# Layer 0 of a four-layer graph network: project the features before they are aggregated, and add a bias as one BF16 product

## The chip, the cores and the metric

The kernel runs on one core of a Trainium2 chip. The metric is the device time of one execution in microseconds (us); lower is better. Three executions of the kernel before took 3515.82, 3516.83 and 3521.38 us; the median is 3516.83 us. Engines are named as in the profile: PE (TensorE, matrix products), PEld (its weight loads), DVE (VectorE), ACT (ScalarE), POOL (GpSimd) and SP (SyncE, whose queue starts all the transfers here).

## The reference

The network has 3327 nodes with 256 features, a dense FP32 adjacency matrix with about 1% nonzero entries, and four residual layers, each followed by a layer norm without weights. Only layer 0 and the entry of layer 1 are touched:

```python
x = _layernorm(x + _L0(x, adj, W))          # W is 256 x 512
def _L0(features, adj, W):
    deg = adj.sum(axis=1, keepdims=True) + 1.0
    neigh = adj @ features / deg
    return jnp.concatenate([features, neigh], axis=-1) @ W.T

x = _layernorm(x + _L1(x, adj, gcn_w, gcn_b, ...))
def _L1(...):
    h = jax.nn.relu(adj @ x @ gcn_w + gcn_b)   # then a layer norm, then a Mamba block over the nodes
```

Layer 2 is a graph attention layer, layer 3 two diffusion steps with top-p attention. Layer 0 is the same as features W1 + (adj features / deg) W2, with W1 and W2 the two halves of W transposed, and since a row's division by deg commutes with a product from the right, also features W1 + (adj (features W2)) / deg.

## The kernel before

The nodes are padded to 26 tiles of 128 (nt = 26). The kernel gives each engine one list of instructions, worked off in order. The framework makes these lists before the run: it goes through the program with estimated durations and takes the ready instruction of highest priority, where earlier in the program means higher priority unless the program says otherwise (high_priority, issue_after, keep_in_program_order). So loads for a later stage can be listed, and run, during an earlier one, if their memory is free. All transfers wait in the one list of SP.

**Layer 0** (lines 162 to 189). xa holds the features of all tiles with a 257th column of ones, so that the product with an adjacency row of tiles also gives the row sums. For each of the 26 output tiles, aggregate() (line 110) multiplies 26 adjacency blocks of 128 x 128 (at, loaded in two pieces of 13 blocks, four buffers) with xa into a PSUM tile acc of 257 columns (line 120). An FP32 product shows as two PE instructions in the profile, so that is 52 instructions a tile. The first tile also loads xa itself, four tiles at a time between the adjacency pieces (lines 115 to 118). Then a chain follows: DVE adds 1 to the row sum (176), takes the reciprocal (177) and scales acc (179) into m; PE transposes m (105), ACT copies it to mt (107); PE multiplies the transposed features xt and mt with the four 128-row blocks of w0 into po (line 183, eight instructions of 256 columns); DVE adds the features (186); layernorm() writes tile it of X0, which is the tile F. After tile 13, projections() prepares small weights of layer 3.

**Layer 1, graph convolution** (convolve(), from line 319). For each of 26 tiles, PE multiplies 26 adjacency blocks with X0 (line 333, 52 instructions); ACT copies the sum (341), PE transposes it (344), ACT copies it (346), PE multiplies with gcn_w (349, four instructions), and adds the bias as a product of a row of ones with the row gcn_b (350): contraction length 1, FP32, two instructions. Then come relu on ACT (353), a norm on ACT and POOL (308 to 316, 360), and a transposition into hT (370, 372). The first three tiles are done ahead of the Mamba block's first chunk, four more ahead of its 16 state steps (pump()), and the other 19 are spread over the later state steps by quotas of work units that the program computes.

**Layer 1, Mamba block.** Chunks of up to 512 nodes; the head of a chunk projects hT (489), does a short convolution (492, 499), silu, and step sizes (513 to 552); 16 state steps with scans on DVE (line 274 in the profile, for all DVE and POOL instructions with a fixed order), exponentials on ACT (281), products on POOL, and sums on PE (624). scratch() hands out the four rotating buffers of a pool that the heads use; the loads of the attention vectors (238) also use it.

Of the kernel before, what the change touches and what calls it, by code (L numbers as in the profile page):

```python
# [9 lines left out]
F32 = mybir.dt.float32  # L10
BF16 = mybir.dt.bfloat16
I32 = mybir.dt.int32
AF = mybir.ActivationFunctionType
ALU = mybir.AluOpType
# [4 lines left out]
P = 128  # L19
D = 256  # L20
EPS = 1e-5
JH = 13
J0 = 4
# [7 lines left out]
NG = DI // P  # L31
DS = 16
DTR = 16
# [14 lines left out]
def gnn_kernel(ctx: ExitStack, tc: tile.TileContext, n: int, a: dict, out: bass.AP):  # L48
    nc = tc.nc
    nt = -(-n // P)  # L50
# [6 lines left out]
    ident = consts.tile([P, P], F32, name="ident")  # L57
# [4 lines left out]
    rdeg = consts.tile([P, nt], F32, name="rdeg")  # L62

    X = keep.tile([P, nt, D], F32, name="X")
# [5 lines left out]
    def load(pool, name):  # L70
        t = pool.tile(list(a[name].shape), F32, name=name)
        nc.sync.dma_start(t, a[name])
        return t
# [20 lines left out]
    def layernorm(dst, y):  # L94
        mv = small.tile([P, 2], F32, name="mv")
        stats(mv, y)
        rs = small.tile([P, 1], F32, name="rs")
        rstd_of(rs, mv[:, 1:2])
        standardize(dst, y, mv[:, 0:1], rs)

    def transposed(pool, psum, src, name):

        pt = psum.tile([P, D // P, P], F32, name="ps")
        for k in range(D // P):
            nc.tensor.transpose(pt[:, k, :], src[:, k * P:(k + 1) * P], ident)
        t = pool.tile([P, D // P, P], F32, name=name)
        nc.scalar.copy(t, pt)
        return t

    def aggregate(atp, psum, it, rhs, cols, jh=JH, source=None):  # L110

        acc = psum.tile([P, cols], F32, name="acc")
        for j0 in range(0, nt, jh):
            m = min(jh, nt - j0)
            if source is not None:
                nc.sync.dma_start(rhs[:, j0:j0 + m, :D], source[:, j0:j0 + m, :])
            at = atp.tile([P, jh, P], F32, name="at")
            nc.sync.dma_start(at[:, :m, :], a["adjT"][it][:, j0:j0 + m, :])
            for j in range(m):
                nc.tensor.matmul(acc, at[:, j, :], rhs[:, j0 + j, :],  # L120
                                 start=(j0 + j == 0), stop=(j0 + j == nt - 1))
        return acc
# [19 lines left out]
    def projections(wpool, psum):  # L142
        w1 = load(wpool, "W1")
        w2 = load(wpool, "W2")
        for h in range(2):
            nc.sync.dma_start(wkq[h][:, :, h * DA:(h + 1) * DA], a["W3"])

        for k in range(2):
            pt = psum.tile([DA, P], F32, name="ps")
            nc.tensor.transpose(pt, w1[:, k, :], ident)  # L150
            wt = wpool.tile([DA, P], F32, name=f"w1t{k}")
            nc.scalar.copy(wt, pt)
            pw = psum.tile([P, DA], F32, name="ps")
            nc.tensor.matmul(pw, wt, w2, start=True, stop=True)
            for h in range(2):
                nc.scalar.copy(wkq[h][:, k, (1 - h) * DA:(2 - h) * DA], pw)

    with tc.tile_pool(name="l1b", bufs=1) as wpool, tc.tile_pool(name="l1at", bufs=2) as l1at:
# [3 lines left out]
        with tc.tile_pool(name="l0", bufs=1) as pool, tc.tile_pool(name="l0w", bufs=2) as work, \  # L162
                tc.tile_pool(name="l0at", bufs=4) as atp, \
                tc.tile_pool(name="l0p", bufs=2, space=PSUM) as psum:
            xa = pool.tile([P, nt, D + 1], F32, name="xa")
            nc.vector.memset(xa[:, :, D:], 1.0)
            for it in range(nt):
                if it:
                    acc = aggregate(atp, psum, it, xa, D + 1)
                else:  # L170
                    acc = aggregate(atp, psum, it, xa, D + 1, J0, a["x"])
                    w0 = load(pool, "w0")
                xt = work.tile([P, D // P, P], F32, name="xt")
                nc.sync.dma_start(xt, a["xT"][:, :, it * P:(it + 1) * P])
                deg = small.tile([P, 1], F32, name="deg")
                nc.vector.tensor_scalar_add(deg, acc[:, D:D + 1], 1.0)
                nc.vector.reciprocal(rdeg[:, it:it + 1], deg)
                m = work.tile([P, D], F32, name="m")
                nc.vector.tensor_scalar_mul(m, acc[:, :D], rdeg[:, it:it + 1])
                mt = transposed(work, psum, m, "mt")  # L180
                po = psum.tile([P, D], F32, name="po")
                for k in range(4):
                    nc.tensor.matmul(po, xt[:, k, :] if k < 2 else mt[:, k - 2, :], w0[:, k, :],
                                     start=(k == 0), stop=(k == 3))
                y = work.tile([P, D], F32, name="y")
                nc.vector.tensor_add(y, po, xa[:, it, :D])
                layernorm(X0[:, it, :], y)
                if it == nt // 2:
                    projections(pool, psum)


        with tc.tile_pool(name="l1aw", bufs=1) as cwork, tc.tile_pool(name="l1c", bufs=2) as ch, \
# [6 lines left out]
            def scratch():  # L199
                return tmp.tile([P, NG, 3 + WC], F32, name="t")  # L200

            gw = load(wpool, "gcn_w")

            w_dt = wpool.tile([32 * (NG - 1) + DTR, P + D + P], F32, name="w_dt")
            gb, one = w_dt[0:1, P:P + D], w_dt[0:1, P + D:]
            nc.sync.dma_start(gb, bass.AP(tensor=a["gcn_b"].tensor, offset=a["gcn_b"].offset, ap=[[0, 1], [1, D]]))
            nc.vector.memset(one, 1.0)

            def by_channel(name):
                t = wpool.tile([P, D // P], F32, name=name)  # L210
                nc.sync.dma_start(t, bass.AP(tensor=a[name].tensor, offset=a[name].offset, ap=[[1, P], [P, D // P]]))
                return t
# [190 lines left out]
            def duty(c, s):  # L403


                m, n, b = tiles_of(c), tiles_of(c + 1), tiles_of(c - 1)
                p = plan(c)
                return 4 * m * (2 if s == 0 else 1) + 24 * (1 <= s <= b) + 16 * len(gates(c, s)) \
                    + 4 * n * len(p["project"].get(s, ())) + 8 * n * (s == p["mixed"]) + 2 * n * len(p["sizes"].get(s, ()))

            def tiles_of(c):
                return (ends[c] - starts[c]) // P if 0 <= c < nch else 0
# [272 lines left out]
            for k, (c, s) in enumerate(states):  # L685
                w = us[c].shape[2]
                m = tiles_of(c)
# [59 lines left out]
                if c and 9 <= s < 9 + tiles_of(c - 1):  # L747
                    rs, nb = plus[:2]
                    i = s - 9
                    x = X[:, starts[c - 1] // P + i, :]  # L750
# [29 lines left out]
                part = min(q, max(0, SPLIT - 4 * m - duty(c, s) // 2)) if len(uses) > 1 else q  # L780
# [7 lines left out]
            m = tiles_of(nch - 1)  # L788
# [5 lines left out]
            for i in range(m):  # L794
                it = starts[nch - 1] // P + i
# [16 lines left out]
    with tc.tile_pool(name="l3", bufs=1) as pool, tc.tile_pool(name="l3d", bufs=1, space=DRAM) as dram:  # L812
# [90 lines left out]
        with tc.tile_pool(name="l2c", bufs=1) as cpool:  # L903
# [5 lines left out]
            with tc.tile_pool(name="l2a", bufs=1) as wpool, \  # L909
# [4 lines left out]
                m = wpool.tile([P, 2], F32, name="m")  # L914
# [5 lines left out]
                one = wpool.tile([2, 1], F32, name="one")  # L920
# [14 lines left out]
                for j0 in range(0, nt, 4):  # L935
                    m = min(4, nt - j0)
# [678 lines left out]
```

## Time and profile before

| | |
|---|---|
| Median of three runs | 3516.83 us |
| Profiled execution, its own time | 3519.38 us |
| Its span, first to last instruction | 3517.5 us |
| Mean granted PE clock | 0.970 |
| PE busy, share of span | 3235.5 us, 92% |
| DVE busy | 2370.4 us, 67% |
| ACT busy | 1740.6 us, 49% |
| POOL busy | 932.8 us, 27% |
| Read from HBM | 294.36 MB |
| PE in layer 0 | from 5.58 us to about 355 us |
| Graph convolutions of layer 1 (line 333) | from 354.1 us to about 1136 us |

A busy share is a mean over stages that have different limits, so the stages are read one at a time. "Idle before" in a group of instructions is the time that the engine stood still just ahead of them, with the instruction that ended most of it. PE records overlap: a product's record is longer than the distance to the next product, and the distance (here called the pitch) is what a stream of products costs.

### The profile page before, as it was taken

Reading aid. Unit: us, or ns where it says so; the run is one execution under the profiler, and the core shown is the slowest. Engines: PE = TensorE matmul, PEld = TensorE weight load, DVE = VectorE, ACT = ScalarE, POOL = GpSimd, SP = SyncE. Lnnn points to the kernel's source line nnn. Section 1 sums busy time; section 2 is a strip of 40 time slices with the busy share of each in tenths; the row PEclk is TensorE's granted clock in tenths of the full one; section 3 lists DMA queues with packets and bytes.
Section 4 is the critical chain, followed back from the end, with each engine's and each line's share of the span. In section 5 each row is a group of like instructions: output and inputs, shape, how many; then the busy total and the mean of one; then the engine's idle time right before and its main releaser. Section 6 shows DMA issues by size and latency. Waiting matters only on the chain. (4 is left out here: it accounts for less than half of the span.)

```text
span 3517.5 us, 43266 instructions
## 1 busy us (share of the span) xinstructions
PE 3235.5 (92%) x15597; PEld 2540.3 (72%) x15597; DVE 2370.4 (67%) x5245; ACT 1740.6 (49%) x2751; POOL 932.8 (27%) x942
## 2 busy tenths in 40 slices
PE   9999988988888766999899999999997999999996
PEld 7888766676676555888677878787775777777775
DVE  1111177999999997777454544444434999999996
ACT  0000356767667675111133333333336888888883
POOL 0000054666665653121100000000001243333332
PEclk9999998999999888999899999999999999999998
DMA  7443334334443222344321212121212112222220
GB/s 248 139 140 110 102 109 112 101 119 106 106 119 91 66 58 92 126 140 145 95 66 56 65 49 65 48 67 47 67 47 74 55 56 67 68 70 61 70 65 16
DMA packets 147577, 307.99 MB, mean 88 GB/s; under 512 B 19570, under 2 KB 68850, under 8 KB 147218
## 3 DMA queue, kind: packets, MB, share of 16 engines
q1 hardware_dynamic: 147346, 305.06, 29.7%
q8 instruction: 126, 2.06, 0.2%
q14 instruction: 105, 0.86, 0.1%
HBM read 294.36 MB, written 10.65 MB: 87 GB/s over the span
## 5 line engine op out<-in xcount | busy, mean ns | idle before, releaser
L274 POOL TENSOR_TENSOR h<-du,row 128x2048 f32<-128x2048 f32 (+1 forms) x110 | 465.7, 4233 | 339.3 <-DVE hc L274 270.8
L274 DVE TENSOR_TENSOR_SCAN h<-dA,carry,h 128x512 f32<-128x512 f32 (+1 forms) x384 | 448.7, 1220 | 19.8 <-ACT dA L281 19.7
L281 ACT ACTIVATE dA<-t,A_log 128x512 f32<-128x512 f32 (+1 forms) x448 | 292.3, 658 | 146.4 <-DVE h L274 143.4
L1058 PE MATMUL acc<-F,at 128*128 128x256 f32 x1352 | 353.5, 387 | 1.0 <-ACT q L832 0.6
L1091 PE MATMUL acc<-X,wt 128*128 128x256 f32 x1352 | 343.5, 390 | 10.5 <-ACT wt L1089 10.2
L1091 PE MATMUL acc<-G,wt 128*128 128x256 f32 x1352 | 336.8, 392 | 6.4 <-ACT wt L1022 5.9
L1091 PEld LDWEIGHTS acc<-X,wt 128*128 128x128 f32 x1352 | 242.6, 189 | 105.3 <-issue 41.3
L120 PE MATMUL acc<-xa,at 128*128 128x257 f32 x1352 | 308.6, 382 | 5.6 <-DMA at<-in_adjT 5.6
L1058 PE MATMUL acc<-X,at 128*128 128x256 f32 x1352 | 308.4, 381 | 0.0
L967 PE MATMUL acc<-F,at 128*128 128x257 f32 x1352 | 303.6, 381 | 1.2 <-DMA U<-in_U 1.2
L333 PE MATMUL cb<-F,at 128*128 128x256 f32 x1196 | 294.0, 394 | 7.4 <-ACT hn L353 4.5
L1091 PEld LDWEIGHTS acc<-G,wt 128*128 128x128 f32 x1352 | 250.1, 193 | 67.0 <-ACT wt L1022 36.8
L1103 DVE MAX8 cand<-e 128x8 f32<-128x128 f32 x676 | 142.2, 278 | 229.0 <-ACT e L1044 217.4
L1058 PEld LDWEIGHTS acc<-F,at 128*128 128x128 f32 x1352 | 237.9, 190 | 75.3 <-issue 50.2
L120 PEld LDWEIGHTS acc<-xa,at 128*128 128x128 f32 x1352 | 255.7, 191 | 42.4 <-issue 5.5
L1058 PEld LDWEIGHTS acc<-X,at 128*128 128x128 f32 x1352 | 252.9, 191 | 40.2 <-issue 7.0
L967 PEld LDWEIGHTS acc<-F,at 128*128 128x128 f32 x1352 | 253.4, 190 | 36.8 <-issue 1.4
L333 PEld LDWEIGHTS cb<-F,at 128*128 128x128 f32 x1196 | 228.8, 197 | 59.4 <-issue 14.3
L624 PE MATMUL y<-ident,hc 128*128 128x128 f32 x1664 | 229.7, 291 | 42.9 <-DVE hc L274 42.3
L624 PEld LDWEIGHTS y<-ident,hc 128*128 128x128 f32 x1664 | 204.5, 151 | 82.5 <-DVE hc L274 59.3
L274 DVE TENSOR_TENSOR hc<-h,row 128x2048 f32<-128x2048 f32 (+2 forms) x114 | 242.8, 2131 | 11.0 <-PE y L624 4.3
L1089 ACT COPY wt<-tp 128x512 f32<-128x512 f32 (+1 forms) x182 | 93.5, 557 | 309.2 <-PE tp L1087 309.0
(352 smaller groups left out, 5264.1 us busy)
## 6 DMA issues: line engine op xcount, KB each, us to landing
at<-in_adjT SPq DMA_DIRECT2D x102, 832.0 KB, 4.6
at<-in_adjT SPq DMA_DIRECT2D x260, 320.0 KB, 2.9
row<-bc SPq DMA_DIRECT2D x80, 512.0 KB, 5.1
at<-in_adjT SPq DMA_DIRECT2D x52, 576.0 KB, 4.0
at<-in_adjT SPq DMA_DIRECT2D x26, 512.0 KB, 3.8
row<-bc SPq DMA_DIRECT2D x32, 384.0 KB, 5.0
xt<-in_xT SPq DMA_DIRECT2D x26, 128.0 KB, 4.1
qd<-q SPq DMA_DIRECT2D x104, 32.0 KB, 1.9
```

What stands on the lines that cost most here:

```text
L120: nc.tensor.matmul(acc, at[:, j, :], rhs[:, j0 + j, :], start=(j0 + j == 0), stop=(j0 + j == nt - 1))
L274: return lambda *x, **k: tc.keep_in_program_order(op(*x, **k))
L281: decays.append(op(*x, **k))
L333: ten.matmul(acc, at[:, j % JC, :], X0[:, j, :], start=(j == 0), stop=(j == nt - 1))
L624: x = ten.matmul(y[:, g * P:(g + 1) * P], h[:, g, i * P:(i + 1) * P], ident, is_transpose=True, start=(first and g == 0), stop=(last and g ...
L967: nc.tensor.matmul(acc, at[:, j, :], F[:, j0 + j, :], start=(j0 + j == 0), stop=(j0 + j == nt - 1))
L1058: nc.tensor.matmul(acc, at[:, j, :], rhs[:, j0 + j, :], start=(j0 + j == 0), stop=(j0 + j == nt - 1))
L1089: copy(wt[:, :m, :], pt[:, :m, :])
L1091: nc.tensor.matmul(acc, wt[:, j, :], rhs[:, j0 + j, :], start=(j0 + j == 0), stop=(j0 + j == nt - 1))
L1103: nc.vector.max(cand[:, s * 8:(s + 1) * 8], z[:, s * SEG:(s + 1) * SEG])
```

## The change

In layer 0, w0 is loaded first, and the identity is added to the two diagonal 128 x 128 blocks of its first half, so that features (W1 + I) already contains the residual. Then a loop ahead of the aggregation loads the transposed features xT in pieces of four tiles (xt, two buffers of 4 KB per partition) and multiplies each tile once with both halves of w0, 512 columns at a time, into a PSUM tile po. DVE copies the first 256 columns to X (a tile that layer 1 overwrites later), ACT copies the other 256 to xa. The aggregation now works on the projected xa; after it, one DVE instruction scales acc by the reciprocal degree and adds X, and the layer norm follows. The features in their plain layout are no longer loaded, and per tile the transposition, its copy, the four products with w0 and the load of xt are gone.

In layer 1, the bias row is split into three BF16 parts, whose sum is the FP32 row, held in partitions 0, 32 and 64 of a tile gb of 65 partitions that is zero elsewhere; the row of ones becomes a 65 x 128 BF16 tile. The line ten.matmul(acc, one, gb, ...) is unchanged in its text and is now a BF16 product of contraction length 65. The split is done once by DVE: two memsets, six copies and two subtractions, on a scratch() buffer into which the bias is loaded for all 65 partitions.

```diff
-    def aggregate(atp, psum, it, rhs, cols, jh=JH, source=None):
+    def aggregate(atp, psum, it, rhs, cols, jh=JH):
 
         acc = psum.tile([P, cols], F32, name="acc")
         for j0 in range(0, nt, jh):
             m = min(jh, nt - j0)
-            if source is not None:
-                nc.sync.dma_start(rhs[:, j0:j0 + m, :D], source[:, j0:j0 + m, :])
             at = atp.tile([P, jh, P], F32, name="at")
             nc.sync.dma_start(at[:, :m, :], a["adjT"][it][:, j0:j0 + m, :])
...
             xa = pool.tile([P, nt, D + 1], F32, name="xa")
             nc.vector.memset(xa[:, :, D:], 1.0)
+            w0 = load(pool, "w0")
+            for k in range(2):
+                own = w0[:, k, k * P:(k + 1) * P]
+                nc.vector.tensor_add(own, own, ident)
+            for j0 in range(0, nt, J0):
+                m = min(J0, nt - j0)
+                xt = work.tile([P, D // P, J0 * P], F32, name="xt")
+                nc.sync.dma_start(xt[:, :, :m * P], a["xT"][:, :, j0 * P:(j0 + m) * P])
+                for i in range(m):
+                    po = psum.tile([P, 2, D], F32, name="po")
+                    for k in range(2):
+                        nc.tensor.matmul(po, xt[:, k, i * P:(i + 1) * P], w0[:, k::2, :], start=(k == 0), stop=(k == 1))
+                    nc.vector.tensor_copy(X[:, j0 + i, :], po[:, 0, :])
+                    nc.scalar.copy(xa[:, j0 + i, :D], po[:, 1, :])
             for it in range(nt):
-                if it:
-                    acc = aggregate(atp, psum, it, xa, D + 1)
-                else:
-                    acc = aggregate(atp, psum, it, xa, D + 1, J0, a["x"])
-                    w0 = load(pool, "w0")
-                xt = work.tile([P, D // P, P], F32, name="xt")
-                nc.sync.dma_start(xt, a["xT"][:, :, it * P:(it + 1) * P])
+                acc = aggregate(atp, psum, it, xa, D + 1)
                 deg = small.tile([P, 1], F32, name="deg")
                 nc.vector.tensor_scalar_add(deg, acc[:, D:D + 1], 1.0)
                 nc.vector.reciprocal(rdeg[:, it:it + 1], deg)
-                m = work.tile([P, D], F32, name="m")
-                nc.vector.tensor_scalar_mul(m, acc[:, :D], rdeg[:, it:it + 1])
-                mt = transposed(work, psum, m, "mt")
-                po = psum.tile([P, D], F32, name="po")
-                for k in range(4):
-                    nc.tensor.matmul(po, xt[:, k, :] if k < 2 else mt[:, k - 2, :], w0[:, k, :],
-                                     start=(k == 0), stop=(k == 3))
                 y = work.tile([P, D], F32, name="y")
-                nc.vector.tensor_add(y, po, xa[:, it, :D])
+                nc.vector.scalar_tensor_tensor(y, acc[:, :D], rdeg[:, it:it + 1], X[:, it, :],
+                                               op0=ALU.mult, op1=ALU.add)
                 layernorm(X0[:, it, :], y)
...
-            w_dt = wpool.tile([32 * (NG - 1) + DTR, P + D + P], F32, name="w_dt")
-            gb, one = w_dt[0:1, P:P + D], w_dt[0:1, P + D:]
-            nc.sync.dma_start(gb, bass.AP(tensor=a["gcn_b"].tensor, offset=a["gcn_b"].offset, ap=[[0, 1], [1, D]]))
+            w_dt = wpool.tile([32 * (NG - 1) + DTR, P], F32, name="w_dt")
+            rows3 = 2 * 32 + 1
+            gb, one = wpool.tile([rows3, D], BF16, name="gb"), wpool.tile([rows3, P], BF16, name="one")
+            nc.vector.memset(gb, 0.0)
             nc.vector.memset(one, 1.0)
+            rest, part = scratch()[:rows3, 0, :D], wpool.tile([rows3, D], BF16, name="part")
+            nc.sync.dma_start(rest, bass.AP(tensor=a["gcn_b"].tensor, offset=a["gcn_b"].offset, ap=[[0, rows3], [1, D]]))
+            for k in range(3):
+                nc.vector.tensor_copy(part, rest)
+                nc.vector.tensor_copy(gb[32 * k:32 * k + 1, :], part[32 * k:32 * k + 1, :])
+                if k < 2:
+                    nc.vector.tensor_sub(rest, rest, part)
```

## The prediction

> **What bounds the kernel now.** I read the page's slices first. PE is at 9 tenths through the first three slices (88 us each) while DVE is at 1, so layer 0 is PE's; from about 600 us DVE is at 9, so the Mamba block is DVE's.
>
> ```profile
> span 3517.5 us, 43266 instructions
> PE   9999988988888766999899999999997999999996
> DVE  1111177999999997777454544444434999999996
> PEclk9999998999999888999899999999999999999998
> ```
>
> Next the timeline of one steady tile of layer 0, PE alone. Columns: start, length of the record, what. PE never stands still, so the pitch is the distance from start to start.
>
> ```profile
> 99.85 1.03 PE L183 MATMUL po<-w,xt 128*128 128x256 f32 x4
> 100.72 0.60 PE L120 MATMUL acc<-xa,at 128*128 128x257 f32 x2
> 101.15 0.38 PE L105 MATMUL ps<-ident,m 128*128 128x128 f32 x2
> 101.37 1.03 PE L120 MATMUL acc<-xa,at 128*128 128x257 f32 x4
> 102.24 1.02 PE L183 MATMUL po<-w,mt 128*128 128x256 f32 x4
> 103.10 10.16 PE L120 MATMUL acc<-xa,at 128*128 128x257 f32 x46
> 113.10 1.03 PE L183 MATMUL po<-w,xt 128*128 128x256 f32 x4
> ```
>
> A tile takes 113.10 - 99.85 = 13.25 us: 52 L120 at (113.10 - 103.10)/46 = 0.217 us are 11.3; eight L183 at 0.217 are 1.73; two transposes 101.37 - 101.15 = 0.22. The chain over DVE and ACT (m, mt) hides behind six L120 of the next tile.
>
> The first tile is not steady; the same view at the start, all engines:
>
> ```profile
> 5.58 13.84 PE L120 MATMUL acc<-xa,at 128*128 128x257 f32 x52 [5.58 <-DMA at<-in_adjT]
> 19.26 0.67 PE L183 MATMUL po<-w,xt 128*128 128x256 f32 x2
> 22.32 11.47 PE L120 MATMUL acc<-xa,at 128*128 128x257 f32 x52
> ```
>
> It waits for its transfers (13.68 us for 52 products instead of 11.3: 2.4 lost), and its chain is exposed (3.06 us instead of 1.95: 1.1 lost). At the other end PE passes to layer 1 without a gap:
>
> ```profile
> 353.26 1.03 PE L183 MATMUL po<-w,xt 128*128 128x256 f32 x4
> 354.12 0.59 PE L333 MATMUL cb<-F,at 128*128 128x256 f32 x2
> 355.64 1.02 PE L183 MATMUL po<-w,mt 128*128 128x256 f32 x4
> 356.50 10.22 PE L333 MATMUL cb<-F,at 128*128 128x256 f32 x46
> ```
>
> Layer 0's last PE work ends at 356.50 with six L333 inside it: 356.50 - 6 x 0.217 = 355.2.
>
> For the bias, a graph convolution's end, and DVE's waits between 400 and 640 us (total, times, longest):
>
> ```profile
> 385.13 1.02 PE L349 MATMUL cb<-gcn_w,m 128*128 128x256 f32 x4
> 386.09 0.69 PE L350 MATMUL cb<-w_dt 1*128 1x256 f32 x2
> 386.71 2.86 PE L333 MATMUL y<-F,at 128*128 128x256 f32 x12
> DVE u L499 <- ACT u L492: 49.9, 1, 49.9
> DVE u L274 <- ACT u L492: 16.9, 1, 16.9
> ```
>
> From 385.13 to 386.71 are 1.58 us; four L349 at 0.217 account for 0.87, so the bias pair costs 0.71, of which 0.43 would be its columns and 0.28 a gap. DVE waits for the head of chunk 0, then of chunk 1, which need convolution tiles 0 to 6: up to about 500 us PE's work is on the path.
>
> **What the Trainium skill says.** "FP8 and Floating Point Precision", TensorE Precision Notes: true FP32 takes four passes through the array, BF16 one. "TensorE: Matmul & The Clock Gate", Back-to-back issue gap: N/2.4 + 2.5 ns, 109 ns for 256 columns. The trace agrees: an FP32 product of 256 columns is two instructions of 0.217 us, four times 109 ns. The same page, "Why this matters for your kernels": a single product of short contraction takes the time of a full one, so 65 rows should be no dearer than one; no run here shows it. It does not price a change between FP32 and BF16, nor does this trace show one.
>
> **The change, part by part.**
>
> *Projection.* 26 tiles x two products of 512 columns = 104 instructions. Instructions of that size are in the trace: four L489 from 504.31 to 506.11 and from 501.74 to 503.45, four L568 from 507.83 to 509.55, 0.43 each. 104 x 0.43 = 44.7 us, against 208 x 0.217 = 45.1 removed: the columns are the same, the gain 0.4.
>
> *Removed on PE.* 52 transposes: 26 x 0.22 = 5.7 us. The m copy on DVE, mt on ACT and DVE's wait for po (59.3 us in total) go as well and are worth nothing: both engines are idle under PE there. What is late next is PE itself, with its 52 products a tile.
>
> *Start.* The first product needs w0 (512 KB) and the first xt (512 KB), 1.0 MB, where before it needed 512 + 256 KB and began at 5.58. The transfers of the first 20 us ran at about 0.37 MB per us, so 0.26 MB more is 0.7: start at 6.3. The two identity additions are at most 0.42 each (a DVE add of twice the width) and lie under the arrival of xt. Bounds: 5.6 to 9.
>
> *Transfers after it.* The third xt waits for a buffer, until four tiles are projected (6.3 + 4 x 1.72 = 13.2), and is needed at 20.1; 512 KB took 5.9 to land under full load. On SP's list the adjacency pieces and layer 1's weights may stand behind it; the earliest needed is at for tile 0, at 51 us. 3.4 MB of plain features go. From then on only at is loaded, 832 KB per 5.6 us, 0.15 MB per us against 0.37: the first tile's 2.4 and 1.1 us are gained.
>
> *Emptying po.* DVE copy about 0.42 (as L186), ACT copy 0.37 (as L107); one after the other still below 1 us, under a 1.72 us fill of the other buffer. Cover is lost if DVE or ACT stands still: in the trace DVE waited 2.0 and 1.9 us for the attention vectors and ACT spent 1.28 on a table load, at 50 to 68 us; such things may now fall into the projection, plus the bias split (ten short DVE operations, some 3 us, and a wait for its load). Each can hold PE for about 1 us. I take 1.5, bounds 0 and 6.
>
> *New tile end.* deg, reciprocal, one DVE operation of about 0.5, norm: about 3 us, behind 50 L333 (10.9 us) even for the last tile. Nothing; acc has two buffers and is free after 1 us.
>
> *Sum of layer 0.* 6.3 + 44.7 + 1352 x 0.217 (293.6) + 1.5 (the small projections at tile 13, whose tile took 14.75 instead of 13.25) = 346.1, against 355.2: -9.1; with 1.5 of stalls -7.6.
>
> *Bias.* One instruction: 0.11, plus the gap of 0.28 or nothing. Not shown; I take 0.25, so 0.46 saved a tile, bounds 0.32 and 0.60 (a loss only if changing the type costs more than 0.6). The seven tiles ahead of the state steps: 3.2, of which I count 2.5, since PE also waits there for the norm's ACT and POOL. For the other 19 (8.7 us of PE) DVE is the bound: between 640 and 1140 us it is busy 475.5 of 500 and waits 2.3 for PE directly and 17 for ACT. I count 1, bounds 0 and 4. The split's DVE time lies in layer 0.
>
> Total: -7.6 - 2.5 - 1 = -11.1. Against the profiled execution's 3519.4 (span 3517.5, 1.9 around it) this gives 3508.3; that execution lies 2.6 above the median, so for the median 3516.8 - 11.1 = **3505.7**.
>
> **Rivals.**
> 1. *The projection is bound by transfers.* If SP's list puts adjacency pieces (four, 3.3 MB) and layer 1's loads (about 4 MB with the first pieces of line 332) ahead of the third xt, 7.3 MB at 0.37 take 20 us from about 5 on, and xt lands at 26 instead of by 20. Against it: each such load in the trace stands in the gap of a waiting at, not in a block. Costs up to 7: about 3513.
> 2. *The bias gives nothing*, because changing type or rows costs a gap as long as the old product, or because the time turns into waits for ACT: -7.6, 3509.2.
> 3. *Slower: the planner's order in layer 1.* The lists are made from estimated durations; a cheaper bias and an earlier layer 1 move the convolution against the heads of chunks 0 and 1, where DVE stood still for 16.9 and then 14.6 us in single waits. If one more convolution tile (about 14.7 us, 383.51 to 398.27) comes ahead of chunk 1's head, and another delays its step sizes, 29 - 11 = 18 us are lost: 3535. The gain is eaten from 11 us of added waits on, and from 18 the loss is measurable. Against it: DVE's and POOL's order there is fixed in the program, and quotas count units, which do not change.
> 4. *The same in the other direction:* one of the two waits shortens by 7: 3499.
>
> **How the numbers follow.** Likeliest case 0.55 (own range 3500 to 3510), rival 1 0.12, rival 2 0.13, rival 3 0.10, rival 4 0.10. About 0.2%, 7 us, is what a measurement of this kernel can tell from no change: below 3509.8 lie nearly all of the likeliest case, rival 4 and half of rival 2, 0.70; rival 3 beyond +0.2% 0.10; the rest 0.20. Range 3495 to 3518: it takes in rivals 1, 2 and 4 and leaves out rival 3.
>
> **What would show it.** In layer 0: 104 products of 512 columns between about 6 and 51 us with no idle time of more than 2 us in all; then starts of L120 11.3 us per tile; first L333 near 346. In layer 1: from the last gcn_w product to the next L333 about 0.25 us instead of 0.71, DVE's two long waits no longer than before, and the 32 state steps after 540 us in the same pattern. I am wrong if PE idles for transfers in the first 50 us, if PE's clock there (1.00 in every 50 us window up to 400) falls, or if the time from the first L333 to the last one of tile 6 grows.

## The result, and the profile after

The changed kernel takes 3509.03 us (median), the kernel before, run beside it, 3521.11 us. The ratio is 0.9968 with a 95% interval of 0.9959 to 0.9976: 11.3 us less, between 8.5 and 14.4. A second comparison, of new executions of both, gave 0.9976 (0.9968 to 0.9984). The profiled execution took 3512.67 us, its span 3510.8.

The page's slices of the kernel after, 88 us each:

```profile
span 3510.8 us, 42847 instructions
PE   9999888988988776999899999999997999999996
DVE  2111168999999997777444444545434999999996
PEclk9999999999999888999899999999999999999998
```

The shape is that of before: PE fills the first three slices, DVE the slices from about 600 us on. DVE's first digit is 2, for the copies out of the projection. Where the time went has to be read from markers along the way, because the two spans differ by only 6.7 us. In us from the start of each span, kernel before and after:

| marker | before | after | difference |
|---|---|---|---|
| layer 0's last product on PE | 355.2 | 350.8 | -4.4 |
| first input product of chunk 0 (w_in) | 405.9 | 399.7 | -6.2 |
| DVE's first convolution tap of chunk 1 | 506.43 | 500.07 | -6.4 |
| first du of chunk 1, the product that DVE's next long series begins with | 578.25 | 567.64 | -10.6 |
| last sum of layer 1 | 1375.5 | 1365.1 | -10.4 |
| first aggregation of layer 2 | 1401.3 | 1391.0 | -10.3 |
| first aggregation of layer 3 | 1743.5 | 1732.5 | -11.0 |
| second half of layer 3 | 2656.6 | 2648.7 | -7.9 |
| end of the span | 3517.5 | 3510.8 | -6.7 |

Two steps make the gain: layer 0 with the first three bias products (-6.2), and a step of 4.2 at the head of chunk 1. The instruction lists of layers 2 and 3 are the same on every engine in both kernels; what moves there is the subject of the last section.

**Layer 0.** The timeline of PE over the first 62 us; columns: start, length of the record, what, and in brackets the idle time ahead and what ended it:

```profile
6.42 15.69 PE L176 MATMUL po<-w,xt 128*128 128x512 f32 x32 [6.42 <-DMA xt<-in_xT]
23.11 17.43 PE L176 MATMUL po<-w,xt 128*128 128x512 f32 x40 [0.99 <-ACT xa L178]
41.00 3.70 PE L176 MATMUL po<-w,xt 128*128 128x512 f32 x8 [0.46 <-ACT xa L178]
45.14 10.57 PE L176 MATMUL po<-w,xt 128*128 128x512 f32 x24 [0.44 <-ACT xa L178]
55.55 6.68 PE L118 MATMUL acc<-xa,at 128*128 128x257 f32 x30
```

The projection begins at 6.42 as forecast (6.3), and no later product waits for a transfer. But it lasts 55.55 - 6.42 = 49.1 us, where 104 instructions of 0.43 are 44.7. Three waits for ACT's copy out of PSUM (the 0.99, 0.46 and 0.44 in brackets) make 1.9 of it. Another 1.7 is at the very beginning. The timeline of all engines, the first 40 us, shows both:

```profile
7.41 0.34 PEld L176 LDWEIGHTS po<-w,xt 128*128 128x128 f32 x1 [0.52 <-issue]
9.12 0.34 PEld L176 LDWEIGHTS po<-w,xt 128*128 128x128 f32 x1 [0.52 <-issue]
9.94 0.19 PEld L176 LDWEIGHTS po<-w,xt 128*128 128x128 f32 x1 [0.49 <-issue]
10.37 0.19 PEld L176 LDWEIGHTS po<-w,xt 128*128 128x128 f32 x1 [0.24 <-issue]
...
20.44 0.29 DVE L212 CAST part<-t 65x256 bf16<-65x256 f32 x1 [1.29 <-DMA t<-in_gcn_b]
...
22.24 0.41 DVE L177 COPY X<-po 128x256 f32<-128x256 f32 x1
22.68 0.37 ACT L178 COPY xa<-po 128x256 f32<-128x256 f32 x1 [3.13 <-DVE X L177]
```

Up to about 9.9 us a weight load takes 0.34 us instead of 0.19, and the loads follow each other at 0.85 (9.12 - 7.41 is two of them) instead of 0.43: the first four instructions run at half rate, 4 x 0.42 = 1.7 us. The longest wait for a copy is the bias split: DVE stands 1.29 us for gcn_b and then does the casts and subtractions from 20.44 on; only at 22.24 does it reach the copy of po's first half. ACT's copy of the second half starts after DVE's, not beside it, and PE gets its buffer last. The other two waits come the same way: DVE stands 1.85 us (until 39.43) and 2.56 us (until 43.57) for the two attention vectors, and the copies of po queue behind it. The remaining 0.8 of the 49.1 is what the restarts cost: by the spacing of the weight loads, each of the three delays the stream by about 0.27 us more than its wait.

The kernel before had this start too. The loads of its first aggregation, in the window from 4 to 8.8 us (smallest, median and largest duration in ns, first and last start):

```profile
L120 PEld LDWEIGHTS acc<-xa,at x9: 286/337/338, 5.5 to 8.7; 128*128 128x128 f32 x9
```

337 ns again, where the median after it is 190; the slow loads go on to 9.99 us, ten steps of 0.43 us from 5.71 instead of 0.217, which is 2.1 us. So of the 2.4 us that the first tile of before took too long, 2.1 were PE's slow start and not a lack of data.

**From there to layer 1.** PE's timeline between 329 and 384 us:

```profile
329.68 21.25 PE L118 MATMUL acc<-xa,at 128*128 128x257 f32 x97
350.77 11.41 PE L341 MATMUL cb<-F,at 128*128 128x256 f32 x52
...
380.05 1.02 PE L357 MATMUL cb<-gcn_w,m 128*128 128x256 f32 x4
380.91 0.27 PE L358 MATMUL cb<-gb,one 65*128 65x256 bf16 x1
381.03 2.76 PE L341 MATMUL y<-F,at 128*128 128x256 f32 x12
```

The aggregation lasts 350.77 - 55.55 = 295.2 us, which is 1352 x 0.217 + 1.5, as computed; there are no transposes and no feature products between the aggregates any more. The bias: from 380.05 to 381.03 are 0.98 us, of which four gcn_w products are 0.87. One BF16 product with 65 rows costs PE 0.11 us, against 0.71 before. That is its columns alone, a quarter of the 0.43 that the columns of the FP32 pair take, with no gap.

**The head of chunk 1.** DVE's waits for ACT, among them those for dA, an input of the state steps; the window before is 354 to 640 us, the window after 350 to 640; columns: total, times, longest. First before, then after:

```profile
DVE h L274 <- ACT dA L281: 25.5, 8, 14.6
```

```profile
DVE u L507 <- ACT u L500: 48.9, 1, 48.9
DVE h L282 <- ACT dA L289: 21.7, 9, 5.9
DVE u L282 <- ACT u L500: 16.9, 1, 16.9
```

The long waits at the heads of chunk 0 (49.9, now 48.9) and of chunk 1 (16.9 in both) stayed. The second wait of 14.6 us, inside chunk 1's head, is no longer there as one piece. DVE's scans in that head, first before, then after:

```profile
543.71 1.80 DVE L274 TENSOR_TENSOR_SCAN h<-dA,h 128x384 f32<-128x384 f32 x2 [14.64 <-ACT dA L281]
571.40 1.80 DVE L274 TENSOR_TENSOR_SCAN h<-dA,h 128x384 f32<-128x384 f32 x2 [3.77 <-ACT dA L281]
```

```profile
526.86 1.95 DVE L282 TENSOR_TENSOR_SCAN h<-dA,h 128x384 f32<-128x384 f32 x2 [4.16 <-ACT dA L289]
536.69 0.96 DVE L282 TENSOR_TENSOR_SCAN h<-dA,h 128x384 f32<-128x384 f32 x1 [3.35 <-ACT dA L289]
560.79 1.80 DVE L282 TENSOR_TENSOR_SCAN h<-dA,h 128x384 f32<-128x384 f32 x2 [5.86 <-ACT dA L289]
```

ACT's timeline of the kernel before shows what the long wait was:

```profile
534.32 0.69 ACT L528 ACTIVATE t<-ps,b_dt 128x512 f32<-128x512 f32 x1 [1.33 <-PE y L527]
...
540.05 0.38 ACT L353 ACTIVATE hn<-cb 128x256 f32<-128x256 f32 x1
...
543.11 1.07 ACT L281 ACTIVATE dA<-t,A_log 128x384 f32<-128x384 f32 x2
```

and ACT's timeline after:

```profile
521.35 0.36 ACT L361 ACTIVATE hn<-cb 128x256 f32<-128x256 f32 x1
...
526.26 0.56 ACT L289 ACTIVATE dA<-t,A_log 128x384 f32<-128x384 f32 x1
...
529.47 0.67 ACT L536 ACTIVATE t<-ps,b_dt 128x512 f32<-128x512 f32 x1
```

Before, ACT did the step sizes of chunk 1 (L528, from 534.32), then the rectifier and norm of a convolution tile (L353), and only then the dA that DVE was waiting for, at 543.11. After, the tile (L361) and the first dA come first, and the step sizes (L536) follow, mixed with further dA. DVE's scans stand 4.16 and 3.35 us instead of 14.64 once, 7.1 less; the wait ahead of du grew from 3.77 to 5.86 and took 2.1 of that back. From the first tap to the first du, chunk 1's head takes 67.6 us instead of 71.8. DVE's own order in layer 1 is the same in both kernels. PE's and ACT's orders changed, and one product of POOL stands in another place. So it is the order that the planner (the framework, as it makes the lists) writes, or else the shorter bias itself; the experiments below separate the two.

### The profile page after: what moved, and what is told of

Its sections match the earlier page's. It is cut to its first block, busy times and chain, and to the rows that moved or that the text cites. A ratio compares the mean times of both kernels' runs of the same rounds, so it can differ in the third digit from the quotient of the medians.

```text
span 3510.8 us, 42847 instructions
## 1 busy us (share of the span) xinstructions
PE 3228.0 (92%) x15415; PEld 2526.5 (72%) x15415; DVE 2374.3 (68%) x5256; ACT 1737.1 (49%) x2749; POOL 932.2 (27%) x942
## 5 line engine op out<-in xcount | busy, mean ns | idle before, releaser
L1099 PE MATMUL acc<-X,wt 128*128 128x256 f32 x1352 | 346.3, 393 | 10.6 <-ACT wt L1097 10.2
L118 PE MATMUL acc<-xa,at 128*128 128x257 f32 x1352 | 294.7, 380 | 0.0
L632 PE MATMUL y<-ident,hc 128*128 128x128 f32 x1664 | 236.9, 297 | 46.2 <-DVE hc L282 46.1
```

The costliest lines, as they stand in the source:

```text
L118: nc.tensor.matmul(acc, at[:, j, :], rhs[:, j0 + j, :], start=(j0 + j == 0), stop=(j0 + j == nt - 1))
L632: x = ten.matmul(y[:, g * P:(g + 1) * P], h[:, g, i * P:(i + 1) * P], ident, is_transpose=True, start=(first and g == 0), stop=(last and g ...
L1099: nc.tensor.matmul(acc, wt[:, j, :], rhs[:, j0 + j, :], start=(j0 + j == 0), stop=(j0 + j == nt - 1))
```

## The experiments

**The changed kernel again, and each part alone.** after_again, layer0_only, bias_only and po3_warm ran on one chip, the other four kernels on another, each beside the kernel before. after_again is the changed kernel unaltered.

> The changed kernel itself, on the same chip as its parts. From its first 20 runs: 0.9968 of the kernel before, 11 us less. By stages of the two traces: end of PE's layer-0 work 4.4 us earlier, first projection of chunk 0 6.2 us earlier, end of layer 1 10.4 us earlier; layers 2 and 3 have the same order of instructions on every engine and should take the same time within 3 us.

layer0_only keeps the bias of before:

```diff
+            w_dt = wpool.tile([32 * (NG - 1) + DTR, P + D + P], F32, name="w_dt")
+            gb, one = w_dt[0:1, P:P + D], w_dt[0:1, P + D:]
...
-            for k in range(3):
-                nc.vector.tensor_copy(part, rest)
...
```

> Only the layer-0 part; the bias stays FP32 with one row. The orders of PE, ACT, DVE and POOL in layer 1 are those of the kernel before. Theory from the two traces: 4.4 us faster (0.9987), all of it before the first graph convolution; the stage from the first product of the graph convolution to the end of layer 1 as long as before within 1 us. The forecast's split: 7.6 us (0.9978). Rival (the earlier loads of layer 1's weights make layer 1 faster): 8 us or more, with layer 1 some 4 us shorter.

bias_only is the kernel before with the new bias block alone (the same diff in the other direction, on the old layer 0).

> Only the bias part; layer 0 as before. The listed orders of PE and ACT in layer 1 are those of the changed kernel. Theory from the traces: 6.2 us faster (0.9982): 1.8 from three convolution tiles at 0.6 each ahead of chunk 0, about nothing from the next four, 4.3 where the head of chunk 1 computes its step sizes, because the order of ACT there is another. DVE's single wait of 14.6 us there is split into waits of 4 to 6. The forecast's split: 3.5 us (0.9990). Rival (price alone, order without effect): 1.8 us.

Measured against the kernel before; the stages are each read from one profile:

| | ratio, interval | layer 0 ends | first w_in product | first tap to du, chunk 1 | layer 1 ends |
|---|---|---|---|---|---|
| before | 1 | 355.2 | 405.9 | 71.8 | 1375.5 |
| after_again | 0.9976 (0.9968 to 0.9984) | 351.3 | 400.4 | 67.5 | 1365.1 |
| layer0_only | 0.9992 (0.9984 to 1.0001) | 351.1 | 401.7 | 72.8 | 1372.4 |
| bias_only | 0.9983 (0.9974 to 0.9993) | 355.4 | 404.2 | 66.1 | 1368.0 |

The parts add up. At the end of layer 1, layer 0 alone gives 3.1 us, the bias alone 7.5, both together 10.4. The bias gives 1.7 by the first input product (three tiles at 0.60 are 1.8) and the rest at chunk 1's head. The traces say why: on PE and ACT, layer0_only has in layer 1 the order of before, instruction by instruction, and bias_only that of after. DVE's timelines show the wait that goes with it, first layer0_only, then bias_only:

```profile
541.12 1.80 DVE L274 TENSOR_TENSOR_SCAN h<-dA,h 128x384 f32<-128x384 f32 x2 [16.09 <-ACT dA L281]
```

```profile
531.16 0.96 DVE L282 TENSOR_TENSOR_SCAN h<-dA,h 128x384 f32<-128x384 f32 x1 [4.17 <-ACT dA L289]
```

The long wait of before (16.09 here) stays with the old bias and is gone with the new one. Layer 0's gain, in contrast, is worth less than what a comparison of whole runs can tell (0.9992, the interval reaches 1.0001).

**What the new bias owes its price to.** Two kernels separate the number of rows from the type. bias_one_row keeps BF16 and puts one row; it leaves out the split, so that two of the three parts of the bias are dropped:

```diff
+            gb, one = wpool.tile([1, D], BF16, name="gb"), wpool.tile([1, P], BF16, name="one")
+            rest = scratch()[:1, 0, :D]
...
+            nc.vector.tensor_copy(gb, rest)
```

> The changed kernel with a BF16 bias product of contraction length 1 instead of 65 (only the first of the three parts of the bias is kept, the split is left out). All orders of PE, ACT and POOL are those of the changed kernel. If the gap of 0.28 around the old bias product came from the short contraction, it is back: from the last gcn_w product to the next convolution product 0.40 instead of 0.12. If it came from FP32, 0.12. By time: at most 7 x 0.28 = 2 us slower than the changed kernel in the first case, equal in the second.

bias_f32_65 keeps 65 rows and stays in FP32, the bias in the first row and zeros in the others:

```diff
+            gb, one = wpool.tile([65, D], F32, name="gb"), wpool.tile([65, P], F32, name="one")
+            nc.vector.memset(gb, 0.0)
...
+            nc.sync.dma_start(gb[0:1, :], ...)
```

> The changed kernel with an FP32 bias product of contraction length 65, the bias in one row and zeros in the others. The orders of PE and ACT in layer 1 are those of the kernel before. If the short contraction made the gap, the pair costs 0.43 instead of 0.71. What decides at the head of chunk 1: if the order does, DVE's single wait of 14 to 16 us is back and the time from chunk 1's first tap to its du is near 72 us as in the kernel before (67.5 in the changed one); if the price of the product does, it lies near 69. By time: 6 us slower than the changed kernel in the first case, 3 in the second.

PE's timelines of the two kernels at the same convolution tile, bias_one_row first:

```profile
380.70 1.02 PE L351 MATMUL cb<-gcn_w,m 128*128 128x256 f32 x4
381.66 0.28 PE L352 MATMUL cb<-gb,one 1*128 1x256 bf16 x1
381.86 2.86 PE L335 MATMUL y<-F,at 128*128 128x256 f32 x12
```

```profile
380.19 1.02 PE L351 MATMUL cb<-gcn_w,m 128*128 128x256 f32 x4
381.06 0.60 PE L352 MATMUL cb<-gb,one 65*128 65x256 f32 x2
381.49 2.76 PE L335 MATMUL y<-F,at 128*128 128x256 f32 x12
```

From the first gcn_w product to the next convolution product, less 4 x 0.217 = 0.87:

| bias product | 1 row | 65 rows |
|---|---|---|
| FP32, two instructions | 0.71 (before) | 1.30 - 0.87 = 0.43 |
| BF16, one instruction | 1.16 - 0.87 = 0.29 | 0.98 - 0.87 = 0.11 |

With 65 rows each costs exactly its columns; with one row each has a gap on top, 0.28 in FP32 and 0.18 in BF16. The gap thus comes with the contraction over a single row, in both types; only its size differs, so the BF16 product of one row took neither of the two prices expected of it (0.40 and 0.12) but 0.29. Going between FP32 and BF16 costs nothing that shows here. No number of rows between 1 and 65 was run.

The same two runs answer the other question, whether the price of the bias or the order shortened chunk 1's head. bias_f32_65 has the order of before and a price of 0.43, bias_one_row the order of after and a price of 0.29:

| | price of the bias | order in layer 1 | first tap to du, chunk 1 |
|---|---|---|---|
| before, layer0_only | 0.71 | before's | 71.8, 72.8 |
| bias_f32_65 | 0.43 | before's | 71.5 |
| bias_one_row | 0.29 | after's | 67.7 |
| after, after_again, bias_only | 0.11 | after's | 67.6, 67.5, 66.1 |
| po3, po3_warm, best (below) | 0.11 | after's | 66.2, 67.6, 67.6 |

Two groups, by order: 71.5 to 72.8 and 66.1 to 67.7. Within each, the price makes no difference beyond the spread of 1.3 and 1.6 us; the step of 4 us lies between 0.43 and 0.29, where the price changes least. So the price does not make it, and the order of ACT, seen above, explains it. That is the reading, not a direct proof: FP32 always comes with the order of before and BF16 with that of after, and a kernel with the old bias in the new order was not run. DVE's timeline of bias_f32_65 still has the long wait, at a bias product 0.28 cheaper than before's:

```profile
538.78 1.80 DVE L276 TENSOR_TENSOR_SCAN h<-dA,h 128x384 f32<-128x384 f32 x2 [14.66 <-ACT dA L283]
```

Whole runs, both with the new layer 0, agree in direction: bias_one_row 0.9958 (0.9944 to 0.9973), bias_f32_65 0.9986 (0.9979 to 0.9992). The up to 2 us that bias_one_row should have lost against the changed kernel are too few to show in whole runs. What in the planner makes a single BF16 instruction in place of a pair come out in this other order was not taken apart; it may well be chance.

**What the projection lost, and whether it can be had back.** Three variants of the changed kernel. po3 gives the projection a third PSUM buffer:

```diff
-                    po = psum.tile([P, 2, D], F32, name="po")
+                    po = psum.tile([P, 2, D], F32, name="po", bufs=3)
```

> The changed kernel with three buffers for po, nothing else; the orders of PE and POOL stay, on ACT and DVE one instruction of layer 0 changes place. The kernel with this and the early products still had one stall of 0.8 us and gained 3.1 us on PE to the end of the projection. Theory: start at 6.4 to 7.4 us with about four products at 0.85, then one stall of at most 1 us: projection in 47.2 us, 1.5 to 2 us less than the changed kernel's 49.1 and 48.7. Rival (the early products did it all): 48.7.

po3_warm has the third buffer and, ahead of the load of w0, products of the identity that nobody reads, to see whether PE's slow start can be moved under the wait for the transfers:

```diff
+            warm = psum.tile([P, P], F32, name="ps")
+            for _ in range(14):
+                nc.tensor.matmul(warm, ident, ident, start=True, stop=True)
```

> The changed kernel with a third buffer for po and 14 products of the identity with itself while PE waits for w0. Theory: the third buffer takes the three stalls of the projection (2.7 us with their restarts), the early products let the first projections run at 0.43 instead of 0.85 us each (1.7 us); 4.4 us faster than the changed kernel, 0.9956 of the one before. Rivals: the half-rate start is not PE's own but that of its operands, then 2.7 only; the early products delay the projection, then slower than the changed kernel by up to 1 us.

best has the third buffer, 12 such products, and the bias split on POOL instead of DVE:

```diff
-                nc.vector.tensor_copy(part, rest)
+                nc.gpsimd.tensor_copy(part, rest)
...
-                    nc.vector.tensor_sub(rest, rest, part)
+                    nc.gpsimd.tensor_tensor(rest, rest, part, op=ALU.subtract)
```

> The changed kernel with three buffers for po, 12 early products of the identity (14 ran until 7.5 us, a little past the arrival of xt), and the bias split moved from DVE to POOL, which is idle in layer 0. Theory: projection from about 6.6 us, 104 products at 0.43 without a stall: 44.8 us; PE's layer-0 work ends 1.7 us earlier than in the kernel with the third buffer and 14 products (348.5), near 346.8; 0.9962 of the kernel before. Rival: POOL holds DVE up, and the stall comes back.

PE's timeline of the first 66 us, po3:

```profile
7.31 37.00 PE L176 MATMUL po<-w,xt 128*128 128x512 f32 x80 [7.31 <-DMA xt<-in_xT]
44.80 10.54 PE L176 MATMUL po<-w,xt 128*128 128x512 f32 x24 [0.49 <-DMA xt<-in_xT]
55.18 11.03 PE L118 MATMUL acc<-xa,at 128*128 128x257 f32 x50
```

With a third buffer no wait for a copy is left, and one of 0.49 us for an xt appears; the projection takes 55.18 - 7.31 = 47.9 us instead of 49.1 (48.7 in after_again). That is less than the 2 us of waits and restarts it removed, because the slow start lasted longer here: loads come at full rate only from 12.39 us on, 5.1 us after the first, which costs 2.4 instead of 1.7. The 47.2 us expected of it were missed by that. PE's timeline of po3_warm:

```profile
1.35 6.34 PE L167 MATMUL ps<-ident 128*128 128x128 f32 x28 [1.35 <-POOL ident masks.py:199]
7.53 12.27 PE L179 MATMUL po<-w,xt 128*128 128x512 f32 x28
20.57 32.88 PE L179 MATMUL po<-w,xt 128*128 128x512 f32 x76 [0.77 <-ACT xa L181]
53.29 12.99 PE L118 MATMUL acc<-xa,at 128*128 128x257 f32 x59
```

The first 28 instructions of the projection now take 12.27 us, 0.43 each plus the end of the last; the half-rate start is gone, and the projection takes 45.8, 2.1 less than in po3. One wait, of 0.77 us, is left. So the slow start is one of PE and not of the projection's operands: products of the identity have it too, and w0 and xt are at full rate after them. best, the same view:

```profile
1.34 5.11 PE L167 MATMUL ps<-ident 128*128 128x128 f32 x24 [1.34 <-POOL ident masks.py:199]
7.54 31.14 PE L179 MATMUL po<-w,xt 128*128 128x512 f32 x72 [1.09 <-DMA xt<-in_xT]
39.25 3.70 PE L179 MATMUL po<-w,xt 128*128 128x512 f32 x8 [0.57 <-ACT xa L181]
43.31 10.54 PE L179 MATMUL po<-w,xt 128*128 128x512 f32 x24 [0.36 <-DMA xt<-in_xT]
```

The first 72 instructions run without a wait; 0.57 and 0.36 come later. Whether moving the split to POOL did that is not shown: po3, with the split on DVE, runs its first 80 without a wait. PE had stood idle for 1.09 us after the early products, and the projection still began at full rate. It takes 46.2 us here; the 44.8 without a stall that were expected, and an end of layer 0 near 346.8, were missed, also because the first xt came at 7.54 us and not at 6.6.

| | ratio, interval | projection | layer 0 ends | layer 1 ends |
|---|---|---|---|---|
| after_again | 0.9976 (0.9968 to 0.9984) | 48.7 | 351.3 | 1365.1 |
| po3 | 0.9961 (0.9946 to 0.9977) | 47.9 | 350.4 | 1364.1 |
| po3_warm | 0.9966 (0.9955 to 0.9977) | 45.8 | 348.5 | 1363.2 |
| best | 0.9957 (0.9943 to 0.9971) | 46.2 | 348.9 | 1364.6 |

The whole times cannot rank these: the intervals overlap each other and that of the changed kernel. best has the lowest ratio of them and the lowest median of all, 3505.17 us beside 3520.32 for the kernel before on its chip. What is shown is the stage: 1.9 to 2.8 us less at the end of layer 0 for po3_warm and best (4.4 over the whole run were expected of po3_warm) than in the two profiles of the changed kernel (350.8, 351.3), of which 0.5 to 1.9 are left at the end of layer 1.

## Why the prediction was right

The forecast was 11.1 us less, with a range of 3495 to 3518 us; measured are 11.3 less by the ratio. The total is right, but three terms of it are off and nearly cancel.

| term | predicted | measured |
|---|---|---|
| layer 0 | -7.6 | -4.4 |
| seven bias products ahead of the state steps | -2.5 | -2.0 |
| head of chunk 1 | 0 | -4.2 |
| the other 19 bias products | -1.0 | +0.2 |
| to the end of layer 1 | -11.1 | -10.4 |

*Start and transfers.* 6.3 was forecast, 6.42 came; xt did not hold PE again. Rival 1, the projection bound by transfers, did not occur. Over the eight profiles of kernels with the new layer 0 the start lay between 6.29 and 7.54, within the bounds; in six of them it was 7.3 or later, so 6.3 is about 1 us early as a rule, and the profile above happened to meet it.

*The projection's price and what PE no longer does.* 0.43 per instruction and 11.3 us per tile were right: from 55.55 to 350.77 the sum holds to 0.1 us, and the transposes are gone. (Of the three stretches that the forecast takes 0.43 from, the one from 504.31 to 506.11 gives 0.45; nothing hangs on it.)

*Layer 0: two terms failed.* It was to end 7.6 us earlier and ends 4.4 earlier. The first error is a misreading of the view that the prediction shows: "It waits for its transfers (13.68 us for 52 products instead of 11.3: 2.4 lost)". 2.1 of these were PE's first products at half rate, a cost that no transfer makes and that the change cannot take away; it came back as 1.7 in the projection. The weight loads, which the forecast did not look at, would have shown it beforehand. The second is the size of the stalls: 1.5 was taken, and 2.7 came (1.9 of waits for the copies and 0.8 of restarts), inside the bounds of 0 to 6 and by the means named there, DVE held up by the bias split and by the attention vectors. 1.7 and 1.2 make 2.9 of the 3.2 missing.

*The bias product.* 0.46 saved was taken, 0.60 measured, the upper bound: neither the change of type nor the 65 rows costs anything. Of the two things left open, the statement of the Trainium skill ("TensorE: Matmul & The Clock Gate", "Why this matters for your kernels") that a single product of short contraction takes the time of a full one holds for 65 rows, and not for one row between full products, which costs 0.18 to 0.28 more. Rival 2, that the bias gives nothing, fell: alone it gives 7.5 us by the end of layer 1. But only 1.7 of them, ahead of chunk 0, are the price that the forecast counted; most of the rest came with the order.

*The tiles.* The first three tiles returned their full 1.8 us (6.2 - 4.4), the next four 0.2: the tap of chunk 1 is ahead by 6.4, where 6.2 and four times 0.60 would be 8.6. The 19 after them gave nothing that shows: from chunk 1's first du to the end of layer 1 are 797.2 us before and 797.5 after. Over the ten profiles this stretch takes 796.0 to 799.4, with no trend by the price, so the 1 us counted for them can be neither confirmed nor ruled out. That DVE is the bound there, as argued, agrees with it.

*The order in layer 1.* Rival 4 said that one of DVE's two long waits could become shorter by 7; the second, of 14.6, turned into 4.2 and 3.4, which is 7.1 less, and after the longer wait ahead of du 4.2 us came through to the path. It occurred together with the likeliest case, not in its place. The table of prices and orders speaks against the price and for the order. Rival 3 is the same mechanism with the other sign, and nothing in the profile of before said which sign would come. Of the 10.4 us at the end of layer 1 some 4.2 are thus, as far as these runs tell, owed to an order that could as well have gone against the kernel; without it some 6.2 us would be left, which is less than the 7 us that the forecast took for the limit of what can be told from no change.

*The range.* On the forecast's own base, 3516.8 x 0.9968 = 3505.6 us, next to 3505.7. With three terms off, that closeness is luck; the range, not the point, is what the working earned.

## What to carry to other kernels

When the first stage is slower than its products' steady pitch, read the weight loads before blaming the transfers: a slow start of the engine looks the same as a wait in the time from the first product to the last, and here products that nobody reads, put under the wait for the first transfer, removed it. A product of one row between full ones cost more here than its columns, and widening it to 65 rows cost nothing and removed the gap. Where the order of work is written from estimates, any change of an instruction's price can reorder other stages by more than it saves, so compare the lists of both kernels before putting a gain down to the operation that was made cheaper.

## What the runs showed that was not expected

**A single row costs more than 65.** 0.71 against 0.43 in FP32 and 0.29 against 0.11 in BF16, as in the table above.

**PE starts at half rate, for 3.5 to 6 us.** From the first weight load to the first at 0.19 us it was 3.5 us (after), 4.8 (before) and up to 6.1 (bias_f32_65, from 6.25 to 12.36). The granted clock gives no hint of it: from 7 to 9 us it reads 1.00 in the kernel after. In po3_warm the early products took all of it. Their weight loads, in the same form as above:

```profile
L167 PEld LDWEIGHTS ps<-ident x28: 287/333/333, 1.3 to 7.1; 128*128 128x128 f32 x28
```

All are slow from 1.3 to 7.1 us, and the projection behind them runs at full rate from its first instructions. A pause of 1.09 us between the two (best) did not bring the slow rate back.

**Layer 2 spreads by itself, and POOL makes the spread.** Its instructions are the same in all the kernels. From its first aggregation to that of layer 3 it took 342.2 us (before), 341.5 (after), 339.9 (after_again), 337.5 (layer0_only), 338.4 (bias_only), 337.6 (po3_warm), 345.1 (po3), 337.8 (best), 337.8 (bias_one_row) and 343.6 (bias_f32_65): 7.6 us between the extremes, more than the gain of layer 0. In the five profiles with 337.5 to 338.4, PE has no wait for POOL between 1435 and 1700 us. In each of the other five, one or two of POOL's instructions for the norm of a tile take 1.3 to 1.7 us longer than for the other tiles (in the kernel before twice some 2.95 us instead of 1.24), and PE stands for their result: 3.7 us in two waits (before), 1.9 (after), 1.9 (after_again), 4.9 (po3) and 4.1 (bias_f32_65). After the waits of po3, bias_f32_65 and after, the granted clock reads 0.50 for 3 to 5 us, which adds 1.7 to 2.5; here, unlike at the start, the record shows the half rate. After the waits of before and after_again (1.7 to 2.0 us) it stays at 1.00. Together this accounts for each profile's excess to within 0.7 us. Why POOL is at times slow, and why a wait of 1.9 us slowed PE in one profile and not in another, stays open.

The first half of layer 3 took 913.1 to 916.8 us. That is why the spans of two profiles (6.7 us apart) say less of this change than the markers in layers 0 and 1.
